# Mamba's convolution moved from VectorE to TensorE, as products with diagonal matrices

## The chip, the core and the metric

The kernel runs on one core of a Trainium2 chip. The core has a TensorE for matrix products (PE; its weight loads are listed as PEld), a VectorE (DVE), a ScalarE (ACT), a GpSimd (POOL) and a SyncE (SP) that issues most DMAs. Each engine takes its instructions in the order in which the program lists them. Products land in PSUM, which has eight banks; everything else works in SBUF. The metric is the device time of one execution in microseconds (us), lower being better. A profile is one execution taken by the hardware profiler. Its span runs from the first to the last instruction that it shows.

## What is computed

The input is `x` of shape (8, 512, 256) in fp32: eight samples of 512 tokens. Four blocks follow each other, each with a residual: a latent attention, a gated feed-forward layer with fp4 quantisation, a bidirectional Mamba block, and the feed-forward layer again. The change touches the Mamba block only:

```python
x = x + attn_a(layernorm(x)); x = x + ffn(layernorm(x))
x = x + attn_b(layernorm(x)); x = x + ffn(layernorm(x))      # attn_b is Mamba

def _causal_depthwise_conv(x, w, b):        # 512 channels, 4 taps each
    ...
def _ssm_dir(xs, conv_w, conv_b, ...):
    xc = silu(_causal_depthwise_conv(xs, conv_w, conv_b))
    ...                                     # dt, B, C from xc; the scan over time
    return y + xc * D_skip
# in attn_b:
xs, z = split(h @ in_w, 2)
y_fwd = _ssm_dir(xs, conv_w, conv_b, ...)
y_back = _ssm_dir(xs[:, ::-1], conv_w_b, conv_b_b, ...)[:, ::-1]
```

A channel's convolution at time t is the sum of four products: its weight k with the input at time t - 3 + k. Channels do not mix. The second direction has weights of its own and looks forward in time.

## The kernel before

One program holds all eight samples. Three generators are interleaved while the program is written out: `thread_a` (attention, up to three samples ahead), `thread_b` (for one step: the Mamba front `mamba_pre` of sample b+1 in alternation with `merge` of sample b-1, then feed-forward layers) and `thread_s` (the state-space work `ssm` of sample b with its preparation `ssm_prep`). Threads a and b are given priority over s. A scheduler then fixes each engine's order from dependences, priorities, free buffers and a model of times; nothing is reordered at run time.

Channels lie on the 128 partitions and the 512 time steps along the free dimension, so a sample's 512 inner channels are four tiles (ND = 4). In `mamba_pre` (L693), for m from 0 to 3, the input projection (L714) puts one tile into a PSUM bank, and ScalarE copies it with its bias into `xs` (L717), a tile with three zero columns on either side, of which there are two. Then, for each of the two directions d, `conv(d, m, xs, xb)` (L681) computes the silu of the convolution and SP stores the tile `xb` to DRAM (`sxc`, L722), from where `ssm_prep` (L776) and `ssm` (L850) load it. The remaining four m (L725 to L730) handle the gate z.

Inside `conv`, ScalarE begins with one tap and the bias (L687); VectorE adds the three other taps (L689); ScalarE takes the tanh of half of it (L690); and VectorE forms (tanh + 1) times the sum (L691), which is twice the silu. The factor 2 is taken back in weights: L670, L671 and L679. All of `conv`'s tiles are of the tag "tmpB", which has three buffers (TC = 3): the result `xb` and the sum `acc`. The gate z (two tiles, L725 and L727) and `merge` (L749, `sz`, one tile, two of them held at a time until the output projection) use the same three.

PSUM has eight banks: "pa" 2 (attention), "po" 1, "pb" 2, "a" 2 (the exponentials of L840) and "y" 1. The "pb" banks serve the feed-forward layers, `mamba_pre`, `merge` (whose sum `mg` stays in one over eight products), `ssm_prep` and the transposes of `ssm`'s result (L861).

The bulk of VectorE's work is `ssm`: for each of 512 steps a product (L837), two scans (L842 forwards, L844 backwards) that read the exponentials from PSUM (L840, ScalarE), a product on POOL (L851), and eight transposing products on TensorE (L854) that sum into bank "y". `h` has four buffers; `rep` has three and is loaded by ScalarE's queue (L819).

`prep_mamba` (L646) runs once at the start. It loads and prepares the weights, among them `cw` (four tap weights per channel) and `cb` (the bias).

Of the kernel before, what the change touches and what calls it, by code (L numbers as in the profile page):

```python
# [10 lines left out]
F32 = mybir.dt.float32  # L11
# [3 lines left out]
AF = mybir.ActivationFunctionType  # L15
ALU = mybir.AluOpType
AX = mybir.AxisListType

P = 128
T = 512  # L20
# [6 lines left out]
ND = INNER // P  # L27
# [35 lines left out]
def tile_hybrid(ctx: ExitStack, tc: tile.TileContext, w: dict, consts: bass.AP, out: bass.AP):  # L63
    nc = tc.nc
    V, S, G, PE = nc.vector, nc.scalar, nc.gpsimd, nc.tensor
# [7 lines left out]
    dr = ctx.enter_context(tc.tile_pool(name="dr", bufs=2, space=bass.MemoryType.DRAM))  # L73
    cnt = [0]
    PB, TB, HB, QB, QA, HT = 2, 3, 3, 2, 2, 1
    LAG, TC, XB = 2, 3, 3
    NHB, NU, NDT, TA, RB, YT = 4, 3, 2, 2, 3, 1

    def const(shape, dt, tag):
        return cp.tile(shape, dt, tag=tag, name=tag)  # L80

    def work(shape, dt, tag, bufs=2):
        cnt[0] += 1
        return wk.tile(shape, dt, tag=tag, name=f"{tag}_{cnt[0]}", bufs=bufs)
# [3 lines left out]
    def psum(tag="pb"):  # L88
        cnt[0] += 1
        return ps.tile([P, 512], F32, tag=tag, name=f"{tag}_{cnt[0]}", bufs=BANKS[tag])  # L90

    def mm(o, L, R, start=True, stop=True, **kw):
        if isinstance(L, tuple):
            PE.matmul(o, L[0], R[0], start=start, stop=False, **kw)
            PE.matmul(o, L[0], R[1], start=False, stop=False, **kw)
            PE.matmul(o, L[1], R[0], start=False, stop=stop, **kw)
        else:
            PE.matmul(o, L, R, start=start, stop=stop, **kw)  # L98
# [8 lines left out]
    def cview(n):  # L107
        o, k = offs[n]
        return cst[:, o : o + k]

    cos_t, sin_t = cview("cos"), cview("sin")
    m8, m4, ident = cview("m8"), cview("m4"), cview("id")
# [523 lines left out]
    Dh = const([P, 2, ND], F32, "Dh")  # L636
    cw = const([P, 2, ND, 4], F32, "cw")
    cb = const([P, 2, ND], F32, "cb")
    TH = T // 2
    xsb = [const([P, 3 + T + 3], F32, f"xs{i}") for i in range(2)]  # L640
    for i in range(2):
# [4 lines left out]
    def prep_mamba():  # L646
        gb = work([P, 2, 2], F32, "gb", 1)
        nc.sync.dma_start(gb[:, 0, :], w["gamma"].rearrange("(a p) -> p a", p=P), allow_slow_non_contiguous=True)
        nc.sync.dma_start(gb[:, 1, :], w["beta"].rearrange("(a p) -> p a", p=P), allow_slow_non_contiguous=True)
        o = psum()  # L650
        win = [work([P, 2 * INNER], F32, "dt", NDT) for _ in range(2)]
        for ct in range(2):
            nc.sync.dma_start(win[ct], w["in_w"][ct * P : (ct + 1) * P, :])
        for m in range(8):
            for ct in range(2):
                PE.matmul(o[:, m : m + 1], win[ct][:, m * P : (m + 1) * P], gb[:, 1, ct : ct + 1],
                          start=(ct == 0), stop=(ct == 1))
        V.tensor_copy(bin_, o[:, :8])
        V.tensor_scalar(binh, bin_, 0.5, None, ALU.mult)
        for ct in range(2):  # L660
            V.tensor_scalar(win[ct], win[ct], gb[:, 0, ct : ct + 1], None, ALU.mult)
            nc.sync.dma_start(win_d[:, :, ct, :].rearrange("m p n -> p m n"), win[ct].rearrange("p (m n) -> p m n", m=8))
        wout = work([P, ND, C], F32, "rep", RB)
        nc.sync.dma_start(wout, w["out_w"].rearrange("(a p) n -> p a n", p=P))
        V.tensor_scalar(wout, wout, 0.5, None, ALU.mult)
        nc.sync.dma_start(wout_d, wout)
        for d, sx in enumerate(("", "_b")):
            wxp = work([P, 2, T], F32, "tmpA", TA).rearrange("p a t -> p (a t)")[:, : ND * 96].rearrange("p (m n) -> p m n", m=ND)
            nc.sync.dma_start(wxp, w["xproj_w" + sx].rearrange("(a p) n -> p a n", p=P))
            V.tensor_scalar(wxp, wxp, 0.5, None, ALU.mult)  # L670
            V.tensor_scalar(wxp[:, :, DTR : DTR + NS], wxp[:, :, DTR : DTR + NS], 0.5, None, ALU.mult)  # L671
            nc.sync.dma_start(wxp_d[d], wxp)
            nc.sync.dma_start(Aneg[:, d], w["A_log" + sx].rearrange("(a p) n -> p a n", p=P))
            nc.sync.dma_start(Dh[:, d, :], w["D_skip" + sx].rearrange("(a p) -> p a", p=P), allow_slow_non_contiguous=True)
            nc.sync.dma_start(cw[:, d], w["conv_w" + sx].rearrange("(a p) k -> p a k", p=P))
            nc.sync.dma_start(cb[:, d, :], w["conv_b" + sx].rearrange("(a p) -> p a", p=P), allow_slow_non_contiguous=True)
        S.activation(Aneg, Aneg, AF.Exp)
        V.tensor_scalar(Aneg, Aneg, -1.0, None, ALU.mult)
        V.tensor_scalar(Dh, Dh, 0.5, None, ALU.mult)  # L679

    def conv(d, m, xs, dst):  # L681
        def tap(k):
            o = k if d == 0 else 6 - k
            return xs[:, o : o + T]

        acc = work([P, T], F32, "tmpB", TC)
        S.activation(acc, tap(3), AF.Identity, bias=cb[:, d, m : m + 1], scale=cw[:, d, m, 3:4])  # L687
        for k in range(3):
            V.scalar_tensor_tensor(acc, tap(k), cw[:, d, m, k : k + 1], acc, ALU.mult, ALU.add)  # L689
        S.activation(dst, acc, AF.Tanh, scale=0.5)  # L690
        V.scalar_tensor_tensor(dst, dst, 1.0, acc, ALU.add, ALU.mult)  # L691

    def mamba_pre(src, scr):  # L693
        xn = work([P, NT, C], F32, "fxn", 1)
# [38 lines left out]
    def merge(scr):  # L733
        for th in range(2):
            tr = slice(th * TH, (th + 1) * TH)
            gt = []
            for mp in range(2):
                mg = psum()
                for k2 in range(0, 8, 2):
                    wp = work([P, FF], F32, "hff", HB)[:, : 4 * P].rearrange("p (a n) -> p a n", a=2)  # L740
                    nc.sync.dma_start(wp, w["merge_w"][k2 * P : (k2 + 2) * P, mp * 2 * P : (mp + 1) * 2 * P].rearrange("(a p) n -> p a n", p=P))
                    yp = work([P, FF], F32, "qv", QB)[:, : 2 * TH].rearrange("p (a t) -> p a t", a=2)
                    nc.sync.dma_start(yp, scr["y"][k2 : k2 + 2, :, tr].rearrange("m p t -> p m t"))
                    for a in range(2):
                        for e in range(2):
                            mm(mg[:, e * TH : (e + 1) * TH], wp[:, a, e * P : (e + 1) * P], yp[:, a, :],
                               start=(k2 + a == 0 and e == 0), stop=(k2 + a == 7 and e == 1))
                    yield
                sz = work([P, 2, TH], F32, "tmpB", TC)  # L749
                nc.sync.dma_start(sz, scr["sz"][2 * mp : 2 * mp + 2, :, tr].rearrange("m p t -> p m t"))  # L750
# [190 lines left out]
    prep_attention()  # L941
    prep_ffn()
    prep_mamba()
    scrs = {}
    def run(*gens):
# [51 lines left out]
```

## Time and profile before

| | |
|---|---|
| time of three runs | 4634.93, 4635.62, 4651.86 us; median 4635.62 |
| profiled execution | 4632.94 us; span 4631.1 us |
| granted TensorE clock, mean | 0.799 of full speed |
| DMA | 896.92 MB, mean 194 GB/s |
| L689, three taps on VectorE | 192 instructions, 208.9 us, mean 1088 ns |
| L691, last product on VectorE | 64 instructions, 59.1 us, mean 923 ns |
| L687, first tap on ScalarE | 64 instructions, 51.7 us, mean 807 ns |
| L690, tanh on ScalarE | 64 instructions, 40.2 us, mean 629 ns |
| L717, copy of the projection | 32 instructions, 21.9 us, mean 683 ns |

Busy times are sums over the span; matrix products overlap each other, so a group's mean is longer than its busy time over its count. A row of a group gives line, engine, operation, output and inputs with shapes, count, then busy us and mean ns of one, then the idle time of the engine just before and what ended most of it. A row of a line gives minimum, median and maximum in ns, first and last start in us. The chain of waits is followed back from the last instruction, at each step to what released it or to the instruction before it on its engine; here it reaches back to 542 us. "Issue" is time for which the profile shows no reason.

### The profile page before, as it was taken

Reading aid. Unit: us, or ns where it says so; the run is one execution under the profiler, and the core shown is the slowest. Engines: PE = TensorE matmul, PEld = TensorE weight load, DVE = VectorE, ACT = ScalarE, POOL = GpSimd, SP = SyncE. Lnnn points to the kernel's source line nnn. Section 1 sums busy time; section 2 is a strip of 40 time slices with the busy share of each in tenths; the row PEclk is TensorE's granted clock in tenths of the full one; section 3 lists DMA queues with packets and bytes.
Section 4 is the critical chain, followed back from the end, with each engine's and each line's share of the span. In section 5 each row is a group of like instructions: output and inputs, shape, how many; then the busy total and the mean of one; then the engine's idle time right before and its main releaser. Section 6 shows DMA issues by size and latency. Waiting matters only on the chain.

```text
span 4631.1 us, 41283 instructions
## 1 busy us (share of the span) xinstructions
PE 3238.4 (70%) x12904; PEld 2009.0 (43%) x12904; DVE 3764.2 (81%) x4599; ACT 1620.6 (35%) x2725; POOL 2066.1 (45%) x925
## 2 busy tenths in 40 slices
PE   4779778777868787768787787656565666566556
PEld 2434344344444454445454454434343444344344
DVE  5335589899699888997888897999899979898873
ACT  1223433533434343433343334333333333333220
POOL 2111344345345454554345543455455545566541
PEclk7779778778878888888888888777777777677658
DMA  5223455656676466754677456654665457567352
GB/s 138 83 83 97 169 191 177 205 197 214 228 246 233 158 232 221 245 198 172 220 238 249 164 170 214 244 188 166 212 237 194 165 212 249 187 238 286 139 202 85
DMA packets 349928, 896.92 MB, mean 194 GB/s; under 512 B 50029, under 2 KB 195726, under 8 KB 284174
## 3 DMA queue, kind: packets, MB, share of 16 engines
q10 hardware_dynamic: 82944, 553.68, 32.6%
q1 hardware_dynamic: 266766, 340.61, 23.2%
q8 instruction: 103, 1.69, 0.2%
q14 instruction: 115, 0.94, 0.1%
HBM read 775.28 MB, written 118.88 MB: 193 GB/s over the span
## 4 chain that ended last, share of the span: by engine, by line
DVE 49%; PE 13%; issue 10%; DMA 10%; POOL 3%; ACT 3%; SPq 0%; ACTq 0%; DVEq 0%; POOLq 0%
DVE h L837 13%; DVE h L844 9%; DVE h L842 8%; PE pb L98 7%; DMA rep<-bcd 4%; POOL h L851 2%; DVE tmpB L689 2%; PE po L474 2%; DVE qv L508 2%; DVE mx L443 2%; PE y L854 1%; PE pa L98 1%; DVE qa L507 1%; DMA tmpB<-ssz 1%; DVE qmx L498 1%
## 5 line engine op out<-in xcount | busy, mean ns | idle before, releaser
L851 POOL TENSOR_TENSOR h<-h,rep 128x1024 f32<-128x1024 f32 x512 | 1376.0, 2688 | 1537.1 <-DVE h L842 448.6
L840 ACT ACTIVATE a<-dt,Aneg 128x512 f32<-128x512 f32 x1024 | 701.8, 690 | 1489.2 <-DVE h L844 758.5
L837 DVE TENSOR_TENSOR h<-u,rep 128x1024 f32<-128x1024 f32 x512 | 889.3, 1740 | 85.7 <-DMA rep<-bcd 43.8
L854 PE MATMUL y<-cst,h 128*128 128x128 f32 x4096 | 663.3, 319 | 368.1 <-POOL h L851 355.6
L854 PEld LDWEIGHTS y<-cst,h 128*128 128x128 f32 x4096 | 567.9, 166 | 493.6 <-POOL h L851 411.8
L844 DVE TENSOR_TENSOR_SCAN h<-a,h 128x512 f32<-128x512 f32 x512 | 598.3, 1204 | 14.0 <-ACT a L840 7.0
L842 DVE TENSOR_TENSOR_SCAN h<-a,h 128x512 f32<-128x512 f32 x512 | 598.2, 1204 | 6.5 <-ACT a L840 1.1
L98 PE MATMUL pb<-wgu,fxT 128*128 128x352 f32 x1024 | 403.1, 532 | 86.9 <-DVE xrf L598 34.3
L474 PE MATMUL po<-pt,vs 128*32 128x128 f32 (+3 forms) x1024 | 351.9, 489 | 22.8 <-ACT pt L469 22.7
L433 PE MATMUL pa<-kst,qst 96*128 96x512 f32 (+3 forms) x512 | 226.5, 493 | 199.4 <-DVE mx L443 96.6
L98 PE MATMUL pb<-qv,hff 128*128 128x256 f32 x1024 | 288.4, 438 | 50.2 <-DMA qv<-sy 22.3
L98 PE MATMUL pa<-xT,wp 128*128 128x512 f32 x512 | 284.4, 689 | 39.8 <-DVE mx L443 27.2
L98 PEld LDWEIGHTS pb<-wgu,fxT 128*128 128x128 f32 x1024 | 209.6, 218 | 222.5 <-issue 43.5
L386 POOL TENSOR_TENSOR tmp<-tmp,tmp 128x512 f32<-128x512 f32 x64 | 95.4, 1491 | 409.7 <-DVE tmp L384 280.2
L469 ACT ACTIVATE pt<-pa 128x512 f32<-128x512 f32 x320 | 185.8, 593 | 251.2 <-PE pa L466 170.3
L98 PEld LDWEIGHTS pb<-qv,hff 128*128 128x128 f32 x1024 | 221.7, 224 | 108.1 <-issue 26.8
L443 DVE TENSOR_REDUCE mx<-pa 128x1 f32<-128x512 f32 (+2 forms) x384 | 179.7, 500 | 105.0 <-PE pa L435 104.5
L464 PE MATMUL pa<-qst,kst 98*128 98x512 f32 (+3 forms) x512 | 215.2, 473 | 63.2 <-ACT pt L469 25.6
L98 PE MATMUL pb<-wdn,hT 128*128 128x256 f32 (+1 forms) x768 | 241.9, 459 | 23.8 <-ACT hT L588 7.8
L433 PEld LDWEIGHTS pa<-kst,qst 96*128 96x128 f32 x512 | 119.2, 233 | 256.8 <-DVE tmp L384 84.1
L689 DVE SCALAR_TENSOR_TENSOR tmpB<-xs,cw,tmpB 128x512 f32<-128x512 f32 x192 | 208.9, 1088 | 20.0 <-ACT tmpB L687 18.1
L98 PE MATMUL pb<-fxT,xrf 128*128 128x512 f32 x256 | 156.1, 742 | 68.2 <-DVE tmpB L751 21.6
(204 smaller groups left out, 4793.0 us busy)
## 6 DMA issues: line engine op xcount, KB each, us to landing
rep<-bcd ACTq DMA_DIRECT2D x512, 1024.0 KB
hld<-hl SPq DMA_DIRECT2D x192, 256.0 KB
hff<-in_merge_w SPq DMA_DIRECT2D x128, 256.0 KB
qv<-sy SPq DMA_DIRECT2D x128, 256.0 KB
kst<-hld SPq DMA_DIRECT2D x64, 384.0 KB
qst<-hld SPq DMA_DIRECT2D x64, 384.0 KB
wp<-wqk_d SPq DMA_DIRECT2D x64, 256.0 KB
sxc<-tmpB SPq DMA_DIRECT2D x64, 256.0 KB
```

Of the source, the lines that this page charges most:

```text
L98: PE.matmul(o, L, R, start=start, stop=stop, **kw)
L433: PE.matmul(o[:, at : at + n], qst[pr][:96, j, i * P : (i + 1) * P], kst[:96, j, :n], start=(k == 0), stop=False)
L443: V.tensor_reduce(M[:, j, i : i + 1], o[:, at : at + n], AX.X, ALU.max, negate=True)
L464: PE.matmul(o[:, at : at + n], kst[:, j, kt * P : (kt + 1) * P], qst[pr][:, j, kt * P :], start=(k == 0), stop=False)
L474: PE.matmul(po[c : c + 32, kt * P :], vs[:, kt, h * VW : h * VW + 32], pt[:, at : at + n], start=(kt == 0), stop=(kt == 2), tile_position= ...
L689: V.scalar_tensor_tensor(acc, tap(k), cw[:, d, m, k : k + 1], acc, ALU.mult, ALU.add)
L837: V.tensor_tensor(h, u[:, m % 2, None, :].to_broadcast([P, 2, T]), rep[:, :, 0, :], ALU.mult)
L840: ex = S.activation(a, dt[:, m % 2, :], AF.Exp, scale=Aneg[:, d, m, 2 * n + e : 2 * n + e + 1])
L842: V.tensor_tensor_scan(h[:, e], a, h[:, e], 0.0, ALU.mult, ALU.add)
L844: V.tensor_tensor_scan(h[:, e, ::-1], a[:, ::-1], h[:, e, ::-1], 0.0, ALU.mult, ALU.add)
L851: G.tensor_tensor(h, h, rep[:, :, 1, :], ALU.mult)
L854: PE.matmul(y[:, i * P : (i + 1) * P], h[:, e, i * P : (i + 1) * P], ident, start=(n == 0 and e == 0 and i == 0), stop=(n == NS // 2 - 1 a ...
```

## The change

For each direction and tile, four diagonal 128 x 128 matrices are made at the start, one for each tap, with the tap's weights on the diagonal: 32 activations on ScalarE, which scale the identity by a column of `cw`. Each group of four (256 KB) is stored to DRAM (`dg_d`). In `conv`, such a group is loaded into a "tmpB" buffer on SP's queue, and TensorE forms the convolution as four products that sum in a "pb" bank, with `xs` shifted by the tap. ScalarE takes the tanh of half the sum out of PSUM, with half of the bias (`cbh`), and then adds 1.0 to it in a second activation. VectorE does one instruction: (sum + bias) times that, with the sum read from PSUM. What is computed stays the same.

```diff
+    cbh = const([P, 2, ND], F32, "cbh")
+    dg_d = dr.tile([2, ND, P, 4, P], F32, tag="dgd", name="dg_d", bufs=1)
...
         V.tensor_scalar(Dh, Dh, 0.5, None, ALU.mult)
+        V.tensor_scalar(cbh, cb, 0.5, None, ALU.mult)
+        for d in range(2):
+            for m in range(ND):
+                dg = work([P, 4, P], F32, "tmpB", TC)
+                for k in range(4):
+                    S.activation(dg[:, k, :], ident, AF.Copy, scale=cw[:, d, m, k : k + 1])
+                nc.sync.dma_start(dg_d[d, m], dg)
 
     def conv(d, m, xs, dst):
-        def tap(k):
-            o = k if d == 0 else 6 - k
-            return xs[:, o : o + T]
-
-        acc = work([P, T], F32, "tmpB", TC)
-        S.activation(acc, tap(3), AF.Identity, bias=cb[:, d, m : m + 1], scale=cw[:, d, m, 3:4])
-        for k in range(3):
-            V.scalar_tensor_tensor(acc, tap(k), cw[:, d, m, k : k + 1], acc, ALU.mult, ALU.add)
-        S.activation(dst, acc, AF.Tanh, scale=0.5)
-        V.scalar_tensor_tensor(dst, dst, 1.0, acc, ALU.add, ALU.mult)
+
+        dg = work([P, 4, P], F32, "tmpB", TC)
+        nc.sync.dma_start(dg, dg_d[d, m])
+        o = psum()
+        for k in range(4):
+            at = k if d == 0 else 6 - k
+            PE.matmul(o, dg[:, k, :], xs[:, at : at + T], start=(k == 0), stop=(k == 3))
+        S.activation(dst, o, AF.Tanh, bias=cbh[:, d, m : m + 1], scale=0.5)
+        S.activation(dst, dst, AF.Identity, bias=1.0)
+        V.scalar_tensor_tensor(dst, o, cb[:, d, m : m + 1], dst, ALU.add, ALU.mult)
```

## The prediction, made before the changed kernel ran

> **What bounds the kernel now.** I read the busy times first, then the chain of waits, then both engines stage by stage, then the rows of the lines that change.
>
> ```profile
> PE 3238.4 (70%) x12904; PEld 2009.0 (43%) x12904; DVE 3764.2 (81%) x4599; ACT 1620.6 (35%) x2725; POOL 2066.1 (45%) x925
> DVE 49%; PE 13%; issue 10%; DMA 10%; POOL 3%; ACT 3%; SPq 0%; ACTq 0%; DVEq 0%; POOLq 0%
> ```
>
> VectorE is the busiest engine and carries half of the chain that ended last. The windows show where (columns: stretch, its length, busy PE, PEld, DVE, ACT, POOL with counts, granted clock, DMA share, GB/s):
>
> ```profile
> 580.00:2900.00 2320.00, 1787.27 (x7427) 1073.97 (x7427) 2028.86 (x2523) 904.67 (x1540) 1078.75 (x486) 0.84 0.60 208
> 2900.00:4408.00 1508.00, 886.85 (x3489) 618.73 (x3488) 1347.18 (x1347) 524.20 (x824) 802.26 (x327) 0.74 0.59 209
> ```
>
> While attention still runs (to about 2900 us) VectorE is busy 87% of the time and TensorE 77%; afterwards 89% and 59%. So the first half has two nearly full engines, the second one. Before 580 us, VectorE is idle half of the time. The convolutions of the eight samples lie in eight stages (436 to 497 us for sample 0, the last 3807 to 3895); summed over these 788 us, the windows give PE 563.9 (72%) and DVE 677.7 (86%).
>
> **What is removed.** The rows of the convolution's lines, and of two lines that read PSUM:
>
> ```profile
> L689 DVE SCALAR_TENSOR_TENSOR tmpB<-xs,cw,tmpB x192: 704/748/2850, 436.3 to 3890.0; 128x512 f32<-128x512 f32 x192
> L691 DVE SCALAR_TENSOR_TENSOR tmpB<-tmpB,tmpB x64: 626/690/2840, 442.1 to 3893.8; 128x512 f32<-128x512 f32 x64
> L862 DVE SCALAR_TENSOR_TENSOR xp<-xp,Dh,pb x64: 643/740/749, 696.5 to 4511.6; 128x512 f32<-128x512 f32 x64
> L384 DVE SCALAR_TENSOR_TENSOR tmp<-pa,bcol,cst x128: 649/741/753, 53.4 to 2771.0; 128x512 f32<-128x512 f32 x128
> L837 DVE TENSOR_TENSOR h<-u,rep x512: 1148/1219/3407, 546.2 to 4497.0; 128x1024 f32<-128x1024 f32 x171
> ```
>
> The three taps (L689) are 192 instructions, 208.9 us, mean 1088 ns although the median is 748. Some take 2.7 us: VectorE then stands beside a POOL product (L851, 2.3 to 2.7 us) that reads SBUF too. The lines with one input in PSUM never exceed 753 ns. The instruction that remains has that form, so I cost it at 0.74 us in place of L691's mean of 59.1 us / 64 = 0.92. VectorE loses 208.9 + 64 x (0.92 - 0.74) = 220 us of work. Of this, 192 x (1.088 - 0.748) + 64 x (0.92 - 0.69) = 80 us is standing beside POOL, and L837 (1148 to 3407 ns) shows that this may reappear at the next instruction; 140 us is certain.
>
> Not all of it was on the path. The chain of waits, asked stage by stage, gives L689 12.8% of 138 us (sample 1), then 8.8, 3.7, 5.1, 5.0, 8.1 and 6.5% of 232 us each: 17.7 + 20.4 + 8.6 + 11.8 + 11.6 + 18.8 + 15.1 = 104 us (the page's 2% of the span agrees). Sample 0 adds nothing: the chain is followed back only to 542 us. L691's shortening, 64 x 0.18 = 12 us, counts half as the taps do: 6. **Gain: 110 us.** Its bounds: 140 / 220 of it, 70, if the blocked time moves to L837; 220 x 0.64 = 141 if VectorE's work passes through at its mean share (its 49% of 4631 us on the chain, 2269, over the 3530 us that it is busy after 542).
>
> On ScalarE two activations go (L687 0.807, L690 0.629 us) and two come: the tanh out of PSUM (like L726, 0.682) and an addition of 1.0 (like L690). That is 64 x (1.436 - 1.311) = 8 us less on an engine busy 35%: 0.
>
> **What is added on TensorE.**
>
> ```profile
> L98 PE MATMUL pb<-fxT,xrf 128*128 128x512 f32 x256 | 156.1, 742 | 68.2 <-DVE tmpB L751 21.6 <-ACT dbt L783 15.6 <-issue 13.0
> 441.67 1.95 PE L98 MATMUL pb<-fxT,xrf 128*128 128x512 f32 x4 [3.21 <-DMA xrf<-win_d]
> 449.04 3.73 PE L98 MATMUL pb<-fxT,xrf 128*128 128x512 f32 x4
> ```
>
> The input projection has the same shape. Its 8 x 8 x 2 = 128 products leave 256 records, two for each; four take 1.95 us at one time and 3.73 at another, so the clock halves. At full clock the weight loads of such a stretch start 0.43 us apart. The convolution's 256 products are 512 records: 512 x 0.43 = 220 us at full clock, 440 at half, 312 by the group's 156.1 / 256 = 0.61 us. At the mean granted clock of 0.80 it is 0.43 / 0.80 = 0.54, so 275 us, which I take. TensorE's work costs the span 13% x 4631 = 602 us on the chain per 3238 busy, 0.19 for one. Outside sample 0 (7/8 of it, 241 us): **+45**; bounds 7/8 x 220 x 0.19 = 37, and, with the 10% of "issue" also on TensorE's account (0.33) and the half clock, 7/8 x 440 x 0.33 = 127.
>
> "TensorE: Matmul & The Clock Gate" in the Trainium skill (Part 1, the clock gate) says that sustained activity releases the throttle, which would speak for the change. This trace agrees in direction: 0.93 granted where PE is busy 108 of 116 us, 0.59 where it is busy 61. If the new bursts kept the gate open, the term would be 37 rather than 45.
>
> **Sample 0** lies where VectorE has slack and TensorE has not (48 of 61 us busy). Eight times four products at 0.86 us are 28 us of TensorE; the taps took 17.9 us of VectorE. State-space work cannot start until it is through. I take **+12**, half-way between 0 (hidden by the other order of work) and 28 less a little.
>
> **What is added in DMA and waits.** Each convolution loads 256 KB of diagonals on SP's queue: 64 x 0.26 = 16.8 MB. DMA carries 10% of the chain, 463 us, for 897 MB: **+9**. The upper bound is that each load is late: the load of the same size (tmpB<-ssz) held the chain for 2.73 us after a 4.63 us store:
>
> ```profile
> 3344.75 2.72 DVE tmpB L689
> 3349.66 4.63 DMA sxc<-tmpB
> 3354.36 2.73 DMA tmpB<-ssz
> ```
>
> 64 x 2.73 = 175 us, half of it on the path: 87. A load waits for one of three "tmpB" buffers, and merge's two gates take two of them. Queued behind it on SP are L711's weights, merge's loads and attention's kst and qst; behind the waiting products on PE are L854's transposes, and behind those, through the four h buffers, L837; behind the tanh on ACT are L840's exponentials, for which the scans wait. Before, the acc buffer needed the same number of slots, but no load. I take the lower end because a load needs no input but the buffer, so it can go while the previous products' tanh runs; that cover is gone when merge holds two.
>
> The sum also stays in one of two "pb" banks from the first product until VectorE's last instruction: 3.4 to 6.9 + 0.68 + 0.63 + 0.74 us and queueing, some 8. "PSUM — Partial Sum Buffer" (Summary: rules for kernel authors) asks to evacuate promptly, and this does not; the rows already show TensorE waiting for pb's readers (L598 36, L573 25, L574 23, L751 42 us). The rule has no price; if the 64 holds of 8 us cost TensorE that much waiting at 0.19, the sum would be 97 us worse, and no longer a gain.
>
> **Preparation**: 32 activations of a 128 x 128 block (0.27 us, like L232) and 8 stores, between 48 and 115 us, where ACT is busy 4.9 of 60 us. 9 us of ACT under attention's start; SP's issues take 8 x 0.4 = 3 us. **+2**; up to 12 if the stores through three buffers hold SP. cbh is one instruction of 0.17 us.
>
> **Sum**: -110 + 45 + 12 + 9 + 2 = -42. The profiled execution took 4632.9 (span 4631.1 and 1.8 around it), 2.7 below the median of 4635.6, so the median becomes about **4594**.
>
> **The rivals.** *TensorE's gain is VectorE's loss (same):* in the eight stages PE would have 564 + 275 = 839 us of work in 788. If the first half (samples 1 to 4, 58.5 of the 104) gives nothing and the +23 of sample 0, DMA and preparation stay, with 45 x 3/7 = 19 of the products in the second half, then -45.5 + 19 + 23 = -3: 4632. For it: 77% before. Against: the clock rises with work. Chance 0.16.
>
> *The convolution becomes a slow chain (slower):* one mechanism, the diagonals' load waiting for tmpB until the previous products have read it. Then the load's upper bound holds, 87 for 9, with the gain at its lower bound of 70: -70 + 45 + 12 + 87 + 2 = +76: 4712. It decides once a convolution starts on average (42 / 64) / 0.5 = 1.3 us late beyond what is hidden. For it: two gates of merge beside it in the same stages, one queue. Against: between the end of a sample's convolutions and its first state step 53 to 140 us lie free (2958 to 3011; 1885 to 2025). Chance 0.38.
>
> *All of VectorE's time comes back:* -141 + 37 + 0 + 9 + 0 = -95: 4541. For it: 89% busy after 2900 us. Against: the chain shows half. Chance 0.10.
>
> *The last instruction is still blocked by POOL*, so that the change does not do what it says: speaks against it that 224 executions with a PSUM input never passed 753 ns. It would give back 12, within the forecast.
>
> **How the numbers follow.** The forecast (4555 to 4612) has 0.36, the larger gain 0.10: faster by over 0.5% (23 us, about what a measurement can tell) 0.46. Same 0.16, slower 0.38. The range is 4505 to 4715: above, the slow chain; below, the large gain and 36 us more, in case L851, which runs 512 x (2.688 - 2.337) = 180 us over its least beside VectorE, gives a fifth of it back.
>
> **What would show it.** L689 gone; the last instruction near 0.74 with none above 0.8; VectorE near 3540 busy; 512 new PE records near 0.54 apart and PE near 3510; L837's mean, 1740 now, higher if the blocked time moved. If ACT's tanh waits for products or PE for the diagonals by more than 80 us in all, or stages from first to last convolution grow beyond 113 us on average (98 now), the slow chain is right and the forecast wrong.

## The result and the profile after

| | before | after |
|---|---|---|
| median of four executions each | 4636.47 us (4634.93 to 4651.86) | 4760.91 us (4757.87 to 4764.65) |
| ratio, 95% interval | | 1.0261 (1.0237 to 1.0285) |
| profiled execution, span | 4631.1 us | 4762.9 us |
| VectorE busy | 3764.2 us | 3542.5 us |
| VectorE idle | 866.9 us | 1220.4 us |
| granted TensorE clock, mean | 0.799 | 0.817 |

The change makes the kernel 2.6% slower. The forecast of 4594 us had the wrong sign, and the time is 46 us above the top of its range. The engine totals and the chain of waits of the changed kernel:

```profile
PE 3413.9 (72%) x13416; PEld 2063.6 (43%) x13416; DVE 3542.5 (74%) x4408; ACT 1619.9 (34%) x2757; POOL 2054.1 (43%) x925
PE 1%; DVE 1%; DMA 1%; POOL 0%; issue 0%; ACT 0%; SPq 0%; DVEq 0%; POOLq 0%; ACTq 0%
```

VectorE's work fell by 222 us, as the sum had it (220). The time rose all the same, so the answer lies in VectorE's idle time, which rose by 353 us. The chain of waits does not help here: it breaks off after a few per cent of the span. The profile's row of the products and the rows by line (minimum, median and maximum in ns, first and last start) show that each new instruction runs as costed:

```profile
L697 PE MATMUL pb<-xs,tmpB 128*128 128x512 f32 x512 | 292.2, 716 | 75.4 <-DMA tmpB<-dg_d 57.2
L700 DVE SCALAR_TENSOR_TENSOR tmpB<-pb,cb,tmpB x64: 685/750/752, 440.4 to 4034.3; 128x512 f32<-128x512 f32 x64
L871 DVE SCALAR_TENSOR_TENSOR xp<-xp,Dh,pb x64: 643/744/749, 703.9 to 4645.4; 128x512 f32<-128x512 f32 x64
L846 DVE TENSOR_TENSOR h<-u,rep x512: 1155/1218/3400, 548.1 to 4629.8; 128x1024 f32<-128x1024 f32 x171
```

The last instruction (now L700) never exceeds 752 ns, and L846 (L837 before) has a mean of 1725 ns where it had 1740: the time blocked beside POOL did not move to it. What is new stands behind the second bar of the product row: of the 75.4 us for which TensorE was idle ahead of the products, 57.2 ended when diagonals had been loaded.

Where the idle time lies is seen in the windows of the eight stages, each from the first copy of a sample's projection (L717, now L726) to the issue of the last store of its convolutions. The last line of that view gives the sums, first of before, then of after:

```profile
sum 783.00, PE 563.77 PEld 345.59 DVE 671.98 ACT 329.76 POOL 285.38; mean PE 70.47 PEld 43.20 DVE 84.00 ACT 41.22 POOL 35.67
```

```profile
1245.00:1403.00 158.00, 129.09 (x505) 73.40 (x504) 95.06 (x124) 66.14 (x109) 60.14 (x24) 0.91 0.67 220
3420.00:3553.00 133.00, 87.83 (x301) 51.39 (x301) 80.63 (x69) 50.06 (x72) 58.07 (x23) 0.82 0.63 223
sum 1057.00, PE 802.46 PEld 443.95 DVE 605.64 ACT 410.06 POOL 397.31; mean PE 100.31 PEld 55.49 DVE 75.71 ACT 51.26 POOL 49.66
```

The stages grew from 783 to 1057 us, and VectorE's idle time inside them from 783 - 672 = 111 to 1057 - 606 = 451 us. Outside them it is nearly the same (757 and 769). In the stage from 3420 us no engine is near full, not even TensorE with 88 of 133 us. So this is not an engine that became the bound but work that waits in turn. The waits of VectorE (us in total, times, longest) show on what, first before, then after:

```profile
DVE tmpB L691 <- ACT tmpB L690: 33.2, 19, 7.2
DVE tmpB L689 <- ACT tmpB L687: 18.1, 11, 3.6
DVE xp L862 <- PE pb L127: 32.4, 16, 10.9
DVE tmpB L729 <- ACT tmpB L728: 28.8, 11, 7.0
DVE tmpA L808 <- POOL dt L807: 22.0, 2, 21.3
```

```profile
DVE xp L871 <- PE pb L127: 115.0, 27, 14.6
DVE tmpB L700 <- ACT tmpB L699: 114.5, 34, 10.7
DVE tmpB L738 <- ACT tmpB L737: 62.0, 17, 7.5
DVE tmpA L817 <- POOL dt L816: 57.9, 15, 12.0
```

Only the second of the after lines is the convolution itself: 114.5 us, where the first two lines of before have 51.3, so 63 us more. The larger part of the new idle time is spent at other work. Within the eight stages, by the same traces, VectorE is idle 95 us at L871 (17 before), 53 at L817 (none) and 35 at attention's L443 (5); L738, the gate z, follows after the stages. L871 waits for transposes that TensorE takes in its order. In the timeline below TensorE first stands 2.2 us for the bank that the L700 of the second direction frees, then runs 36 records of other products, of which the first 16 are shown, and only then these transposes.

One convolution in the timeline of after (start, duration, instruction, in brackets the idle time of its engine before it and what ended that):

```profile
3420.20 2.34 DVE L851 TENSOR_TENSOR_SCAN h<-a,h 128x512 f32<-128x512 f32 x2
3424.45 5.83 PE L697 MATMUL pb<-xs,tmpB 128*128 128x512 f32 x8 [2.85 <-ACT tmpA L810]
3430.32 0.69 ACT L698 ACTIVATE tmpB<-pb,cbh 128x512 f32<-128x512 f32 x1 [5.92 <-PE pb L697]
3431.04 0.63 ACT L699 ACTIVATE tmpB<-tmpB 128x512 f32<-128x512 f32 x1
3431.70 0.75 DVE L700 SCALAR_TENSOR_TENSOR tmpB<-pb,cb,tmpB 128x512 f32<-128x512 f32 x1 [9.16 <-ACT tmpB L699]
3432.51 1.12 PE L808 MATMUL pb<-dbt,wdt 65*128 65x512 f32 x2 [2.22 <-DVE tmpB L700]
...
3442.43 5.39 PE L98 MATMUL pb<-qv,hff 128*128 128x256 f32 x16 [2.23 <-DVE tmpB L700]
...
3454.03 0.75 DVE L871 SCALAR_TENSOR_TENSOR xp<-xp,Dh,pb 128x512 f32<-128x512 f32 x1 [8.98 <-PE pb L127]
```

Read it downwards: TensorE takes 5.8 us for the four products, ScalarE has stood 5.9 us for them, then come two activations, and VectorE, which ended its scans at 3422.5, has stood 9.2 us at L700 for an instruction of 0.75 us. As soon as L700 has read the bank, TensorE goes on with a product that needed that bank (L808). Before the change VectorE's three taps needed only `xs` and the tap that ScalarE had begun with (L687), for which VectorE stood 18.1 us in all.

### The profile page after: what moved, and what is told of

It reads as the page before. It is cut to its first block, busy times and chain, and to the rows that moved or that the text cites. A ratio compares the mean times of both kernels' runs of the same rounds, so it can differ in the third digit from the quotient of the medians.

```text
span 4762.9 us, 42265 instructions
## 1 busy us (share of the span) xinstructions
PE 3413.9 (72%) x13416; PEld 2063.6 (43%) x13416; DVE 3542.5 (74%) x4408; ACT 1619.9 (34%) x2757; POOL 2054.1 (43%) x925
## 5 line engine op out<-in xcount | busy, mean ns | idle before, releaser
L860 POOL TENSOR_TENSOR h<-h,rep 128x1024 f32<-128x1024 f32 x512 | 1362.0, 2662 | 1569.9 <-DVE h L853 458.2
L846 DVE TENSOR_TENSOR h<-u,rep 128x1024 f32<-128x1024 f32 x512 | 881.0, 1725 | 129.5 <-DMA rep<-bcd 68.5
L863 PE MATMUL y<-cst,h 128*128 128x128 f32 x4096 | 632.0, 309 | 319.1 <-POOL h L860 305.5
L863 PEld LDWEIGHTS y<-cst,h 128*128 128x128 f32 x4096 | 543.1, 161 | 428.7 <-POOL h L860 354.0
L851 DVE TENSOR_TENSOR_SCAN h<-a,h 128x512 f32<-128x512 f32 x512 | 597.5, 1205 | 24.5 <-ACT a L849 16.2
L697 PE MATMUL pb<-xs,tmpB 128*128 128x512 f32 x512 | 292.2, 716 | 75.4 <-DMA tmpB<-dg_d 57.2
L474 PE MATMUL po<-pt,vs 128*32 128x384 f32 (+3 forms) x1024 | 333.4, 475 | 11.5 <-ACT pt L469 11.3
L98 PE MATMUL pb<-qv,hff 128*128 128x256 f32 x1024 | 269.7, 417 | 54.3 <-DMA qv<-sy 41.4
L443 DVE TENSOR_REDUCE mx<-pa 128x1 f32<-128x512 f32 (+2 forms) x384 | 179.6, 500 | 132.5 <-PE pa L435 132.3
L98 PEld LDWEIGHTS pb<-qv,hff 128*128 128x128 f32 x1024 | 206.4, 210 | 108.5 <-DMA qv<-sy 38.7
L98 PEld LDWEIGHTS pb<-wdn,hT 128*128 128x128 f32 (+1 forms) x768 | 165.0, 230 | 101.4 <-issue 29.8
L697 PEld LDWEIGHTS pb<-xs,tmpB 128*128 128x128 f32 x512 | 113.8, 234 | 211.5 <-issue 164.9
```

What stands on the lines that cost most here:

```text
L474: PE.matmul(po[c : c + 32, kt * P :], vs[:, kt, h * VW : h * VW + 32], pt[:, at : at + n], start=(kt == 0), stop=(kt == 2), tile_position= ...
L697: PE.matmul(o, dg[:, k, :], xs[:, at : at + T], start=(k == 0), stop=(k == 3))
L846: V.tensor_tensor(h, u[:, m % 2, None, :].to_broadcast([P, 2, T]), rep[:, :, 0, :], ALU.mult)
L851: V.tensor_tensor_scan(h[:, e], a, h[:, e], 0.0, ALU.mult, ALU.add)
L860: G.tensor_tensor(h, h, rep[:, :, 1, :], ALU.mult)
L863: PE.matmul(y[:, i * P : (i + 1) * P], h[:, e, i * P : (i + 1) * P], ident, start=(n == 0 and e == 0 and i == 0), stop=(n == NS // 2 - 1 a ...
```

## The experiments

Times are of one execution unless a count is given. The kernel before read 4654 to 4656 us in its single executions beside them, and 4636 to 4662 us in the sessions with more (medians 4650 and 4652), so single differences under 20 us are not read. VectorE's busy and idle times, and the stages, are summed from each kernel's trace as above; span = busy + idle in the stages + idle elsewhere, in every row.

| kernel | time | VectorE busy | stages | idle in them | idle elsewhere |
|---|---|---|---|---|---|
| before | 4636 (4 executions) | 3764 | 782 | 110 | 757 |
| after | 4761 (4) | 3543 | 1059 | 452 | 769 |
| e1_pa_all | 4823 | 3533 | 1002 | 391 | 898 |
| e2_pa_late | 4727 | 3532 | 1015 | 405 | 789 |
| e3_one_pass | 4670 | 3563 | 907 | 355 | 750 |
| e4_no_load | 4684 | 3526 | 900 | 345 | 812 |
| e5_prep_again | 4678 (6) | 3761 | 779 | 125 | 789 |
| e6_act_empties | 4800 | 3586 | 1072 | 438 | 775 |
| e7_before_plus_products | 4681 | 3744 | 776 | 138 | 797 |
| e8_wp | 4870 | 3523 | 955 | 394 | 951 |
| v1_made_by_act | 4766 | 3565 | 991 | 425 | 775 |
| v2_made_by_act_one_pass | 4674 | 3533 | 870 | 331 | 809 |
| b1_one_buffer | 4724 | 3540 | 1016 | 347 | 835 |
| b2_buffer_no_load | 4690 | 3547 | 962 | 370 | 771 |
| v3_act_one_pass_one_buffer | 4576 (4) | 3557 | 870 | 250 | 767 |
| v4_act_one_buffer_fp32 | 4637 (10) | 3526 | 964 | 314 | 788 |
| v5_pa_late | 4538 (4) | 3543 | 780 | 236 | 759 |

**The bank that the sum holds.** The first theory was that one of two "pb" banks, held from the first product to VectorE's instruction (9.1 us on average in the trace of after), blocks everybody else. Two kernels put the sum into attention's banks, for all samples and for the last three, for which attention was expected to be over (in after it ends at 2796 us, and their stages begin at 2930).

```diff
-        o = psum()
+        o = psum("pa")                                  # e1_pa_all
+        o = psum("pa" if fronted[0] > 5 else "pb")      # e2_pa_late, fronted counts samples from 1
```

> The convolution's sum goes to a pa bank, not a pb bank. Theory 'bank' (with merge's sum in one pb bank, the other is passed on serially, and each convolution holds it until VectorE's last instruction): the stages of samples 5 to 7, when attention is over and pa is empty, shrink from 132, 133 and 130 us to 105 or less; those of samples 1 to 4 by less, since attention uses pa; time 4640 +- 40. Theory 'load' (the diagonals arrive late) and theory 'TensorE time' (the products themselves fill the stages): stages within 8 us of after, time 4760 +- 20.

> As the last, but only for samples 5 to 7, whose convolutions begin when attention is over, so that nothing is taken from attention. Bank: their stages 105 us or less, the others as in after, time 4760 - 3 x 27 = 4680 +- 20. Load or TensorE time: no change, 4760 +- 15.

Measured 4822.67 and 4726.69. With "pa" for all, attention is held up instead: idle elsewhere rises by 129 us. For the last three samples alone it gains 34 us, and their stages become 130, 116 and 117 us where they were 132, 133 and 130. The first of these stages shrinks least, and there the expectation did not hold: in this kernel's own order the last sample's attention runs from 2956 to 3255 us, over that stage (2902 to 3032), and it does so in e1_pa_all too (until 3353). The bank is a link of the chain, and smaller than the first theory said. A third kernel let ScalarE copy the sum out of the bank, so that VectorE reads SBUF:

```diff
+        acc = work([P, T], F32, "tmpB", TC)
+        S.activation(acc, o, AF.Identity, bias=cb[:, d, m : m + 1])
...
-        S.activation(dst, dst, AF.Identity, bias=1.0)
-        V.scalar_tensor_tensor(dst, o, cb[:, d, m : m + 1], dst, ALU.add, ALU.mult)
+        V.scalar_tensor_tensor(dst, dst, 1.0, acc, ALU.add, ALU.mult)
```

> ScalarE copies the sum with its bias into a tmpB buffer and takes the tanh; VectorE's last instruction reads SBUF alone, so that the pb bank is free before VectorE comes to it (held 1.8 + 0.75 us shorter by the trace of after). Bank as a large part: 4710 +- 20. If the tmpB buffers are the tighter resource, the third buffer that this needs costs more than the bank gives: 4780 or more.

Measured 4799.74, as its second theory had it: the third "tmpB" buffer for each convolution costs more than the bank's earlier release gives. With one execution, 39 us above after, this is a likely reading and not more.

**The diagonals' load.** In e4_no_load the products read the identity, which lies in SBUF, instead of the loaded diagonals, so the taps are left out of the convolution; neither load nor buffer is needed then.

```diff
-        dg = work([P, 4, P], F32, "tmpB", TC)
-        nc.sync.dma_start(dg, dg_d[d, m])
...
-            PE.matmul(o, dg[:, k, :], xs[:, at : at + T], ...)
+            PE.matmul(o, ident, xs[:, at : at + T], ...)
```

> The diagonals are not loaded: the identity, which lies in SBUF, stands for all four taps, so the convolution is left out of what is computed and the products' number and shape stay. Load: TensorE's 57 us of waits for diagonals go and the slot waits with them, stages together from 1058 to 900 us or less, time 4690 or less. Bank: only those 57 us, half of them on the path, time 4735 +- 20. TensorE time: 4760 +- 15.

Measured 4684.34, 77 us less than after. The products' row in its profile:

```profile
L695 PE MATMUL pb<-xs,cst 128*128 128x512 f32 x512 | 269.4, 676 | 26.9 <-ACT tmpA L808 14.4
```

The wait for the load is gone from it, 75.4 us of idle time ahead of the products have become 26.9. Load or buffer? One kernel loads into attention's "wp" buffers instead (its tag "wp" in place of "tmpB").

> The diagonals are loaded into attention's weight buffers (wp, two of 2 KB) instead of tmpB. If the load is late because it waits for a tmpB buffer, most of the 77 us that leaving it out gave come back: 4700 +- 20, the late stages near 117 us. If the load's own time or the queue is what costs: 4755 +- 20.

Measured 4870.07, worse than either theory had it: as with e1_pa_all, attention is delayed (idle elsewhere 951). Its last three stages, 128, 118 and 124 us, lie between the 117 of the first theory and the 130 to 133 of after, so its time decides nothing on the load. The question came back with the kernels further down.

**The products' time.** With operands in the format fp32r, which lowers the convolution's precision, TensorE shows one record for each product instead of two.

```diff
-    xsb = [const([P, 3 + T + 3], F32, f"xs{i}") for i in range(2)]
+    xsb = [const([P, 3 + T + 3], FPR, f"xs{i}") for i in range(2)]
...
-        dg = work([P, 4, P], F32, "tmpB", TC)
-        nc.sync.dma_start(dg, dg_d[d, m])
+        dg = work([P, 4, P], FPR, "tmpB", TC)
+        nc.sync.dma_start(dg.bitcast(F32), dg_d[d, m])
```

> The products run with fp32r operands, one record for each product in place of two: 256 records, half of TensorE's added time, at lower precision. TensorE time: stages 1 to 4, where TensorE is busy 81%, shrink by 15 us or more each, stages 5 to 7 (66%) hardly; time 4690 +- 20. Bank: the bank is held 2.4 us shorter by each convolution, in the late stages as well: 8 x 2.4 = 19 us less in each stage, time 4640 +- 30. Load: 4760 +- 15.

Measured 4670.38, 91 us less, where the ranges of the two theories that expected a gain meet. The stages of the last three samples shrink too (132, 133, 130 to 110, 114, 114 us), although TensorE was a third idle there. So the products count by standing in the chain, not only by filling TensorE. The counterpart: the kernel before with four products for each convolution whose sum nobody reads.

```diff
+        o = psum()
+        for k in range(4):
+            PE.matmul(o, ident, tap(k), start=(k == 0), stop=(k == 3))
         acc = work([P, T], F32, "tmpB", TC)
```

> The convolution of before, and beside it four products of the new shape for each convolution (with the identity, no load) whose sum nobody reads. Chain: the products cost only TensorE's time, at the prediction's price of 0.19 some 50 us: 4690 +- 25, and VectorE's idle time in the stages stays near the 110 us of before. Rival 'TensorE time' (its load alone makes the loss): 4740 or more.

Measured 4681.08, 27 us above the kernel before beside it; the stages do not grow (776 us), and VectorE idles 138 us in them. TensorE's work alone costs 27 us or less, since the new order of the rest (below) can do as much by itself; the same products with VectorE behind them cost far more.

**The order of the rest.** The kernel before with the diagonals made and stored at the start, read by nobody; and with the one unused instruction for `cbh`:

```diff
+        for d in range(2):                              # e5_prep_only, e5_prep_again
+            for m in range(ND):
+                dg = work([P, 4, P], F32, "tmpB", TC)
...
+                nc.sync.dma_start(dg_d[d, m], dg)
...
+        V.tensor_scalar(cbh, cb, 0.5, None, ALU.mult)   # n1_cbh_only
```

> The convolution of before; only the diagonals' making and storing at the start is added, and nobody reads them. Theory 'chain' (each convolution is now a serial chain of buffer, load, products, two activations and VectorE, and the fixed order lets VectorE stand through it): 4640 +- 12. Rival 'order' (any added instruction upsets the planned order, and the loss is nothing of the convolution's): 4690 or more.

> The kernel before with the diagonals made and stored at the start, read by nobody, a second time, now in several executions, since a single one was 41 us above the kernel before and single executions of that kernel differ by up to 17. Order theory (the preparation shifts the fixed order for good): 4675 to 4700. Rival (an effect of a first execution): 4655 or less.

> The kernel before with one more VectorE instruction at the start (half of the convolution's bias, 128 x 8 values) whose result nothing reads. By its work it costs about 0.1 us. Theory (the loss is a chain of waits in each convolution, and the order of the rest gives a little of it): 4655 +- 15 beside the kernel before run in the same session. Rival (any change of the program shifts the order that is fixed beforehand by 40 us or more, and what the preparation alone cost was that): 30 us or more away from the kernel before, in either direction.

Measured 4694.67 once, then 4677.52 as a median of six against 4650.23: ratio 1.0057 (1.0036 to 1.0077), so 17 to 36 us. The unused instruction: 4659.16 beside 4655.57, nothing that a single execution tells. In the trace of the latter VectorE, ScalarE and GpSimd run the same instructions in the same order as before, with the one added, so it does not test the rival that any change moves the order. With the preparation the order on all three differs from the start on. The preparation therefore has a real effect, far above its own work. Up to the fourth sample the state-space work starts when it did (2154 us against 2153), and only then does it fall behind (2725 against 2705); why is open. Differences of up to some 40 us between two kernels (e2, e6, e7, b1, v5 against v3) are about as large as what such a new order did here, and show little by themselves; those of e3, e4, b2, v3 and v4 against after are 71 us and more.

**The priority of the last instruction.** VectorE's instruction was given the state-space work's priority.

```diff
+        with tc.high_priority(offset=-1000):
             V.scalar_tensor_tensor(dst, o, cb[:, d, m : m + 1], dst, ALU.add, ALU.mult)
```

> The changed kernel with VectorE's last instruction of the convolution given the priority of the state-space work instead of one 1000 places ahead, so that state-space instructions that are ready by the plan stand in front of it. Nothing else changes. Theory (the loss is VectorE standing at an instruction whose sum is not ready while later work is): VectorE's idle time in the stages falls from 452 to 380 or less and the time to 4715 +- 25. Rival (the bank is the tighter place: a sum that is read later holds one of two banks longer): 4760 or more.

Measured 4764.79. This tells nothing on its question: in the two traces, each of the 64 instructions has the same number of state-space products ahead of it on VectorE, so its place did not move. Read as a repetition of after, it agrees with it within 4 us.

**Buffer or latency.** ScalarE makes the four diagonals in the buffer at each convolution, in fp32 (v1) and in fp32r (v2); nothing is prepared or loaded.

```diff
         dg = work([P, 4, P], F32, "tmpB", TC)
-        nc.sync.dma_start(dg, dg_d[d, m])
+        for k in range(4):
+            S.activation(dg[:, k, :], ident, AF.Copy, scale=cw[:, d, m, k : k + 1])
```

> The changed kernel without the stored diagonals: at each convolution ScalarE makes the four diagonals in the tmpB buffer, so that no load stands in the chain, but the buffer and four short activations do. All of the computation is done. Theory (a chain in which the load's latency was worth 77 us when taken out whole): 4700 +- 25, the stages from a sample's first to last convolution 900 to 980 us in all. Rival 1 (the tmpB buffer itself, not the load's latency, is what is waited for): 4740 or more, stages above 1000. Rival 2 (the preparation at the start costs 40 us by its effect on the order, on top of the chain): 4660 or less.

> As the kernel in which ScalarE makes the diagonals, with the convolution's operands in the format that TensorE takes in one pass (fp32r), which lowers their precision. Chain theory: the load's 77 us and the products' 91 us are shares of one chain and add up in good part, so 4620 to 4660, stages 800 to 880 us in all, VectorE's idle time in them below 290. Rival (the two overlap: whichever is shortened, the bank, the buffer or the order keeps the rest): 4670 or more.

Measured 4766.36 and 4674.46: no gain over the kernels with the load (4761, 4670), though the preparation is gone too. Both theories of a chain missed (4700 +- 25 and 4620 to 4660), and the times are those of the first rival and of the rival that saw the two overlap. One activation takes 388 ns, so four take 1.6 us in place of a load. Two more kernels separate the buffer from what fills it: b1 keeps the load, and writes tanh and result into the diagonals' own buffer (one buffer for each convolution instead of two); b2 has no load but keeps the second buffer, with one activation in place of four, and all four products read that one matrix.

```diff
# b1_one_buffer
+        dst = dg.rearrange("p a k -> p (a k)")
         S.activation(dst, o, AF.Tanh, bias=cbh[:, d, m : m + 1], scale=0.5)
# b2_buffer_no_load
-        nc.sync.dma_start(dg, dg_d[d, m])
+        S.activation(dg[:, 0, :], ident, AF.Copy, scale=cw[:, d, m, 3:4])
```

> The changed kernel with one tmpB buffer for each convolution instead of two: the tanh, the activation behind it and VectorE's instruction write into the buffer that held the diagonals, which the products have read by then. The load stays, all of the computation is done. Buffer theory (what leaving out the load saved was the buffer, since making the diagonals in the buffer without a load saved nothing): 4700 or less, stages from first to last convolution 930 us or less in all, VectorE's idle time in them 370 or less. Rival (the load's latency or TensorE's time in the chain): 4740 or more, stages above 1000.

> The changed kernel without the load, but with its buffer: one short activation writes one 128 x 128 matrix into the buffer, and all four products read that one, so the convolution's taps are replaced. Beside the kernel without load and buffer (4684) it has the buffer back, beside the one in which ScalarE makes all four diagonals (4766) it has three activations less for each convolution. Buffer theory: 4735 or more. Rival (ScalarE's four activations, about 1 us in the chain, took the place of the load's latency): 4705 or less. Between them: a share each.

Measured 4723.71 and 4690.22. The buffer theory expected 4735 or more of b2 and falls: the buffer costs next to nothing when it is filled in 0.4 us (4690 against 4684 without it). Freeing a buffer with the load kept gives 37 us, less than the theory's 61. In b1 the stages (1016 us) stay as long as the rival said, and VectorE's idle time in them (347 us) is as low as the theory said. A reading that fits all four kernels, and that none of them shows by itself, is that the links are tied: what counts is the time from a free buffer to filled diagonals, and with a second buffer that time can be hidden in part.

**The chain shortened.** All three steps together (v3: made by ScalarE, one buffer, fp32r; the result has a lower precision), then at full precision (v4), then v3 with attention's bank for the last three samples (v5, where the last sample's attention again runs late, from 2819 to 3085 us).

```diff
# v3: in conv, from the changed kernel
-        dg = work([P, 4, P], F32, "tmpB", TC)
-        nc.sync.dma_start(dg, dg_d[d, m])
+        dg = work([P, 4, P], FPR, "tmpB", TC)
+        for k in range(4):
+            S.activation(dg[:, k, :], ident, AF.Copy, scale=cw[:, d, m, k : k + 1])
...
+        dst = dg.rearrange("p a k -> p (a k)")
# v4: the same with F32 for FPR; v5: v3 and the bank of e2_pa_late
```

> Three shortenings together: ScalarE makes the diagonals (no load, nothing prepared at the start), operands in the one-pass format, and one tmpB buffer for each convolution; the convolution and its result have a lower precision. Buffer theory: beside the 4674 without the last step it gains 30 us or more: 4600 to 4645, about as fast as the kernel before or a little faster. Rival (the chain through bank, activations and VectorE's place in the order keeps the rest, whichever of its parts is shortened): 4660 to 4690.

> As the kernel with all three shortenings (4576), but with full fp32 operands, two records of TensorE for each product again: all of the computation is done at its full precision. Chain theory: the products' longer time was worth about 91 us where it was shortened alone, and what it costs here lies between that and 60: 4630 to 4670, within 1% of the kernel before. Rival (one buffer and no load are enough, the products then hide): 4600 or less, a gain at full precision.

> The kernel with all three shortenings, and the convolution's sum in attention's bank for the last three samples, whose attention is done. Bank theory (the same step gave 34 us in the changed kernel, where 9 us of bank were held for each convolution): with shorter holds 10 to 30 us, so 4545 to 4570. Rival (with the chain short the bank is no longer what is waited for): within 8 us of 4576.

| kernel | median | before beside it | ratio, 95% interval |
|---|---|---|---|
| v3_act_one_pass_one_buffer | 4576.19 | 4650.23 | 0.983 (0.9797 to 0.9862) |
| v4_act_one_buffer_fp32 | 4637.01 | 4652.06 | 0.9978 (0.9962 to 0.9994) |
| v5_pa_late | 4538.36 | 4652.06 | 0.9762 (0.9736 to 0.9787) |

v3 is faster than any theory had it, v4 lies in the range of the chain theory, and the 38 us from v3 to v5 are a little above the bank theory's 10 to 30. The same idea, with VectorE's work as low as in the changed kernel (3543 us both), is 2.4% faster than before in v5, and at full precision about level in v4. The timeline of v5, in the stage that answers to the one shown of after:

```profile
3259.37 2.11 PE L691 MATMUL pa<-xs,tmpB 128*128 128x512 f32 x8
3265.19 1.25 ACT L693 ACTIVATE tmpB<-pa,cbh 128x512 fp32r<-128x512 f32 x2
3269.57 1.13 ACT L694 ACTIVATE tmpB<-tmpB 128x512 fp32r<-128x512 f32 x2
3272.23 0.74 DVE L695 SCALAR_TENSOR_TENSOR tmpB<-pa,cb,tmpB 128x512 fp32r<-128x512 f32 x1
3272.89 2.42 DVE L844 TENSOR_TENSOR h<-u,rep 128x1024 f32<-128x1024 f32 x1
3275.23 0.74 DVE L695 SCALAR_TENSOR_TENSOR tmpB<-pa,cb,tmpB 128x512 fp32r<-128x512 f32 x1
```

The products of both directions are done in 2.1 us as soon as the projection is copied, since both sets of diagonals lie ready; ScalarE has no idle time before the tanh, nor VectorE before its instruction, and its other work (L844) goes on in between. Not every convolution goes so: v5 still waits 77.2 us in all ahead of this instruction, where after waits 114.5.

## Why the prediction was wrong, point by point

**The work on VectorE: right.** 220 us less was worked out and 222 came, at the duration taken from the rows with an input in PSUM. (The 2.7 us given there as the longest L851 is its mean; the longest took 4.4.)

**"Gain: 110 us": the step that failed.** It gave back the taps' share of the chain of waits. That share says what the taps cost, not what takes their place when they go, and for the wait of what takes their place the sum had, outside sample 0, the 9 us for the load and nothing else. The taps needed `xs` and ScalarE's first tap (18.1 us of standing in all); the instruction that stays has a buffer, a load, eight records of TensorE and two activations ahead of it, and VectorE takes its instructions in a fixed order. Its idle time in the stages rose by 341 us, more than the 222 that were saved: 63 at the convolution's own instructions, the rest at other work of the same stages. v4 shows how much the rest weighs. It stands 101.8 us at the convolution's instruction (after: 114.5), but 51.7 at the transposes' result (115.0) and 20.2 at the counterpart of L817 (57.9), and at full precision it takes the time of before. How the convolution holds up the other work is read from the timeline; a kernel in which only VectorE's instruction comes later in the order was not obtained (the change of priority did not move it). Shortening the chain shows that the gain is there and is lost to this: with the same VectorE work, v5 idles 236 us in the stages instead of 452 and runs 223 us faster.

**"I take the lower end because a load needs no input but the buffer" (9 us): wrong.** Without the load 71 (b2) to 77 us (e4) come back, near the upper bound of 87, as long as nothing takes its place: v1, in which ScalarE makes all four diagonals instead, gets nothing back. The buffer for which the load waits was named, but its cover was assumed to hold. Giving the load a buffer earlier (b1) is worth 37.

**The slack of 53 to 140 us "against" the slow chain: read wrongly.** The starts of state-space work used there were spaced evenly; the trace has 2153, 2705, 3202 us and so on, so the gaps from the second sample on are 155 to 281 us, and 147 to 250 after. Even this larger slack did not help. A sample's convolutions are in no hurry; VectorE loses time on the previous sample's work while it stands at them. Slack of the transferred work covers nothing if engines wait for it in order.

**TensorE's products, 45 us:** as work alone at most 27 (e7, one execution), which does not tell 45 from less. As a link, halving them was worth 91 (e3). The predicted distance of 0.54 us between records was right (within a convolution the weight loads start 0.54 us apart on average); the engine's total rose by 176 us, not 275, since other products took less (the scan's transposing products 632 us where they had 663).

**The bank, left out of the sum:** 8 us were estimated for each convolution and 9.1 measured, and only the sum by the rule of "PSUM — Partial Sum Buffer" in the Trainium skill (Summary: rules for kernel authors), to evacuate promptly, counted it. That sum was a loss, and the runs agree with its sign: relief for three of eight samples gave 34 us (e2), and 38 in the shortened kernel (v5 against v3), though in both the last sample's attention moved as well. But the bank is not what v4 relieved: there it is held 9.6 us on average, as long as in after, and the kernel is 124 us faster.

**Sample 0, 12 us:** its stage grew from 62 to 73 us, but its state-space work started 2 us later (548 against 546), so 2. **Preparation, 2 us, at most 12:** 17 to 36 by e5_prep_again; not its work, which delays no state-space work up to the fourth sample, but, as far as the traces tell, its effect on the order.

**The rival "the convolution becomes a slow chain" (4712)** was the right one, too small: it held the load alone, and kept a gain of 70. It had been given 0.38, more than the forecast's own 0.36. Its signs came out as written: 135.2 us of ScalarE's tanh waiting for products and 57.2 us of TensorE waiting for diagonals (more than 80 together), and stages of 132 us on average (over 113). ScalarE's wait for the products is a sign and no measure: it falls from 135 us in after to 95 in b1, 84 in e4, 57 in e3 and 39 in v4, but v2 has 19 and takes 4674 us, and v5 has 41 and is the fastest. v1 has 78 and is as slow as after, and there TensorE waits for ScalarE instead. Who waited for ScalarE to make the diagonals (us, times), in v1, then in v4:

```profile
PEld pb L691: 39.2, 24
PE pb L691: 30.0, 11
```

```profile
PEld pb L691: 7.7, 12
PE pb L691: 4.7, 3
```

**What stays open.** The shares do not add. One buffer is worth 37 us with the load (after to b1), but 129 when ScalarE makes the diagonals (v1 to v4); making them instead of loading gives nothing with two buffers and 87 with one (b1 to v4). The rows of v1 and v4 just above fit an explanation that was not tried by itself: with one buffer for each convolution the next diagonals are made ahead of need. Attention's bank was not tried at full precision. The order is planned anew for each kernel, and its own effect, 17 to 36 us in the one case measured, is in every difference above. Against the two rivals of equal or better time (4632, 4541) speaks the whole result.

## What to carry to other kernels

Moving work off the busiest engine pays only if the instruction that stays there is ready when its turn comes: count the links ahead of it (buffer, load, products, activations) and ask who stands in order behind each, before crediting the saved time. Such links are worth attacking together, by making operands in place, by reusing a buffer that has just been read and by a bank that nobody else wants: here a loss of 2.6% became a gain of 2.4%, of which 0.2% was reached at the convolution's full precision (v4) and the rest with a lower one and attention's bank. A share of the chain of waits is a price of what stands there now, not a credit for what replaces it.

## What the runs showed of the hardware

An fp32 product of 128 x 128 by 128 x 512 shows two records, an fp32r product one: v5's eight products above took 2.11 us, while in after four took 5.83 us at one time and 3.60 at another. In the long case most weight loads started 0.85 us apart, in the short one 0.43. The granted clock was 0.50 over the first 4.1 us of the long case and 1.00 in the short one, though its mean over that stage was 0.82: the clock was halved for TensorE just where ScalarE and VectorE stood waiting (neither was busy in these 4.1 us).

Making a 128 x 128 diagonal on ScalarE, with a scale for each partition, took 385 to 390 ns (medians of five kernels), where the copy of the same shape used for the estimate (L232, out of PSUM and without such a scale) takes 266.
